# Sums of the moving operand by accumulating DMAs: the last product of an RWKV attention and Hadamard feed-forward kernel

## The chip, the cores and the metric

The kernel runs on one core of a Trainium2 chip. A core has TensorE (PE in the profile) for matmuls, VectorE (DVE), ScalarE (ACT), GpSimd (POOL) and SyncE (SP), which here only issues DMAs. Data live in SBUF, 128 partitions wide; matmuls write into PSUM, eight banks of 128x512 fp32. DMA engines move data between HBM and SBUF, or within SBUF. The engines run their own instruction queues in order and meet at semaphores. The metric is the device time of one execution in microseconds, lower is better; where several executions are known, their median.

## The reference

The input x is 4 x 2048 x 512. It is normalised over channels. An RWKV-v4 attention mixes each token with the one before, forms r, k, v by three 512x512 products, runs the WKV recurrence along time, and multiplies sigmoid(r) * wkv by Wo. A feed-forward forms silu(xn W1) * (xn W3), 2048 wide, applies a Walsh-Hadamard transform to it, and multiplies by W2. Both are added to x:

```python
    hidden = jax.nn.silu(up_gate) * up_lin
    hidden = fwht(hidden)
    out = jnp.einsum('bsh,dh->bsd', hidden, W2)
    ...
    x = x + _L0_attn_ref(xn, ...) + _L0_ffn_ref(xn, L0_ffn_W1, L0_ffn_W2, L0_ffn_W3)
```

All is fp32.

## The kernel before, in words

Tokens are worked in eight blocks of 1024 (`TB`), each in two halves of 512 (`H`). Channels lie on the partitions. A block has three stages: the projections r, k, v, the feed-forward's first two products (`up`, sixteen tiles), and the last product (`down`). The Hadamard transform is folded into W2 once, in the first block (`fold_products`, `fold_butterflies`), so that `down` is one product: the 2048 hidden channels and the 512 channels of sigmoid(r) * wkv, stacked, against W2 and Wo, stacked. The two summands of the output thus come out of the same accumulation.

Each large product uses a scheme with seven block products instead of eight. Its operands are cut into quarters: the weights by halves of input and output channels, the moving operand into y11, y12, y21, y22, by halves of the input channels (first index) and of the tokens (second). The scheme needs sums and differences ("forms") of quarters on both sides. The weights' seven forms are made once by GpSimd (`seven_forms`), stored in HBM (`down_w`), and loaded again for each block (`load_down`, two buffers). The moving operand's forms are made in each block, in place.

In `down`, the moving operand lies in `hid` (sixteen rows of 128 channels) and `r_sb` (four rows). A quarter is a list of pieces: eight rows of `hid`, by twos, and two rows of `r_sb`, one token half of each (`rows`, line 488). A product (`product`, line 498) runs two output tiles of ten 128x512 fp32 matmuls; the profile records each as two. The tuple `order` (line 494) tells which weight form each of the seven products uses. `difference` (line 515) makes the moving operand's forms on VectorE, five subtractions each, in place: y11 becomes y12 - y11 after product 0, y12 becomes y22 - y12 and y22 becomes y22 - y11 between products 2 and 4, y21 becomes y21 - y22 after that. Other VectorE and ScalarE instructions read the banks, add residuals of x from SBUF slots (`stage`, in v_sb; `x22_of`, in e1), and SP stores the results (`store`, line 526).

The order of every engine's queue is the order in which the program issues its instructions: the wrapper `InOrder` (line 24, through which all instructions get line 34 in the profile) keeps it. While `down` runs, the generator `next_tokens` (line 689) prepares the next block, one step ahead of each product: statistics of the new tokens (with a power function on GpSimd, line 130, and a way through HBM), the normalisation (`normalize`, line 145, half of it on GpSimd), the token mixing (`mixed`) and its forms. The loads of the next weight form are issued by SP at the start of each product (line 502) and those of residuals between them.

The final steps of `wkv` (line 221) leave sigmoid(r) * wkv in r_sb; the last instructions of an `up` tile (lines 414 to 419) leave the hidden values in `hid`.

Of the kernel before, what the change touches and what calls it, by code (L numbers as in the profile page):

```python
# [10 lines left out]
ALU = mybir.AluOpType  # L11
# [4 lines left out]
H = 512  # L16
# [23 lines left out]
def tile_rwkv_attn_hadamard_ffn(  # L40
# [15 lines left out]
    NT, C = x.shape  # L56
    F = 2 * w2.shape[1] * P
    NB = C // P
    KH = NB // 2
    NF = F // P  # L60
# [28 lines left out]
    def bank():  # L89
        turn[0] += 1  # L90
        return banks[(turn[0] - 1) % 8]
# [126 lines left out]
            act.copy(dst, pt)  # L218


    def wkv(h):
        w_h, u_h = weff[:, h : h + 1], vec[:, 4, h : h + 1]
        r, k, v = r_sb[:, h, :], k_sb[:, h, :], v_sb[:, h, :]
        a0, a1, b0, b1 = sa[:, OFF - 1 : OFF - 1 + TB], sa[:, OFF : OFF + TB], sb[:, OFF - 1 : OFF - 1 + TB], sb[:, OFF : OFF + TB]
        first_a, first_b, last_a, last_b = a0[:, 0:1], b0[:, 0:1], a1[:, TB - 1 : TB], b1[:, TB - 1 : TB]
        tt, stt, scan, copy = dve.tensor_tensor, dve.scalar_tensor_tensor, dve.tensor_tensor_scan, dve.tensor_copy
        cy = [carry[:, h, n : n + 1] for n in range(3)]

        def exp(t):
            act.activation(t, t, AF.Exp)  # L230


        copy(first_a, cy[0])
        scan(a1, w_h.to_broadcast([P, TB]), k, first_a, ALU.add, ALU.max)
        tt(b1, k, a1, ALU.subtract)
        yield
        stt(e1b, a0, w_h, a1, ALU.add, ALU.subtract)
        stt(e1, k, u_h, a0, ALU.add, ALU.max)
        stt(k, k, u_h, e1, ALU.add, ALU.subtract)
        tt(e1, a0, e1, ALU.subtract)  # L240
        copy(cy[0], last_a)
        yield
        exp(b1)
        exp(e1b)
        yield

        copy(first_a, cy[1])
        tt(a1, b1, v, ALU.mult)
        scan(a1, e1b, a1, first_a, ALU.mult, ALU.add)
        copy(cy[1], last_a)  # L250
        yield
        exp(k)
        exp(e1)
        yield
        copy(first_b, cy[2])
        scan(b1, e1b, b1, first_b, ALU.mult, ALU.add)
        copy(cy[2], last_b)
        tt(v, k, v, ALU.mult)
        yield
        num, den = e1, e1b  # L260
        tt(den, e1, b0, ALU.mult)
        tt(den, den, k, ALU.add)
        dve.reciprocal(den[:, 0:H], den[:, 0:H])
        yield
        dve.reciprocal(den[:, H:TB], den[:, H:TB])
        yield
        tt(num, e1, a0, ALU.mult)
        tt(num, num, v, ALU.add)
        stt(r, r, 1.0, num, ALU.add, ALU.mult)
        stt(r, r, 0.5, den, ALU.mult, ALU.mult)  # L270
        yield


# [64 lines left out]
    def seven_forms(t, a11, a12, a22, a21):  # L338

        sub = ALU.subtract  # L340
        pool.tensor_tensor(t[1], a21, a22, ALU.add)
        pool.tensor_tensor(t[2], t[1], a11, sub)
        pool.tensor_tensor(t[3], a12, t[2], sub)
        pool.tensor_tensor(t[0], a11, a21, sub)

    def forms_in(t):
        seven_forms([t[:, n] for n in range(3, 7)], *(t[:, n] for n in range(4)))

# [47 lines left out]
    def up(i, j, w, tail, step):  # L396

        keep_parts(i, 3 * KH + j, w)
        h0, h1 = hid[:, j, 0:H], hid[:, j, H:TB]

        def on11(pa):
            act.activation(h0, pa, AF.Tanh, scale=0.5)

        def on22(pa, pb, s5):
            dve.scalar_tensor_tensor(h0, h0, 1.0, pa, ALU.add, ALU.mult)
            step()
            dve.tensor_tensor(pb, pb, s5, ALU.add)

        def on12(pc, s5):
            dve.tensor_tensor(pc, pc, s5, ALU.add)  # L410
            step()

        pb, pc, pd = seven(f"{i}_{j}", w, right_of["up"], tail, on11, on22, on12)
        return (
            lambda: act.activation(h1, pc, AF.Tanh, scale=0.5),
            lambda: dve.tensor_tensor(h0, h0, pd, ALU.mult),
            lambda: dve.scalar_tensor_tensor(h1, h1, 1.0, pc, ALU.add, ALU.mult),
            lambda: dve.tensor_tensor(h1, h1, pb, ALU.mult),
        )


# [22 lines left out]
    def fold_butterflies():  # L444

        at, spare = list(fold), e1
        s = 1
        while s < NP:
            for a in range(NP):
                if a & s:  # L450
                    continue
                xa, xb = at[a], at[a | s]
                dve.tensor_tensor(spare, xa, xb, ALU.subtract)
                dve.tensor_tensor(xa, xa, xb, ALU.add)
                at[a | s], spare = spare, xb
            s *= 2
        for a in range(NP):
            x0, x1 = at[a][:, 0:C], at[a][:, C : 2 * C]
            dve.tensor_tensor(spare[:, 0:C], x0, x1, ALU.add)
            dve.tensor_tensor(spare[:, C : 2 * C], x0, x1, ALU.subtract)  # L460
            at[a], spare = spare, at[a]
        return sorted(enumerate(at), key=lambda p: p[1] is not e1)

# [6 lines left out]
    def down_forms(j, at, t):  # L470
        n, a = at[j] if j < NP else (j, None)
        far = down_w[:, :, n].rearrange("f p k c -> p f k c")
        if n < NP:
            a = a.rearrange("p (k m g c) -> p k m g c", k=2, m=2, c=P)
            seven_forms([t[:, f] for f in range(4)], a[:, 0, 0], a[:, 1, 0], a[:, 1, 1], a[:, 0, 1])
            sp.dma_start(out=far[:, 0], in_=a[:, 0, 0])
            sp.dma_start(out=far[:, 1:3], in_=a[:, 1])
            sp.dma_start(out=far[:, 3:7], in_=t[:, 0:4])
        else:
            forms_in(t)  # L480
            sp.dma_start(out=far, in_=t)

    def load_down(i, form):
# [4 lines left out]
    def rows(kh, half):  # L488

        n = NF // 2  # L490
        pieces = [hid[:, kh * n + 2 * a : kh * n + 2 * a + 2, ts(half, H)] for a in range(n // 2)]
        return pieces + [r_sb[:, kh * KH : (kh + 1) * KH, ts(half, H)]]

    order = (0, 1, 4, 6, 5, 3, 2)

    def down(i, w, between, w_after, last):
        y11, y12, y21, y22 = rows(0, 0), rows(0, 1), rows(1, 0), rows(1, 1)
        def product(k, pts, right, start, then):
            if k == 6:
                w_after()  # L500
            elif k:
                w.append(load_down(i, order[k + 1]))
            if k:
                next(between)
            for g in range(KH):
                whole = slice(0, H)
                for pt, cols in ending if last and k == 6 and g == KH - 1 else [(pts[g], whole)]:
                    for n in range(NR):
                        pe.matmul(
                            pt[:, cols], lhsT=w[k][:, n, g, :], rhs=right[n // 2][:, n % 2, cols],  # L510
                            start=start and n == 0, stop=n == NR - 1, skip_group_check=True,
                        )
                    then(g) if cols == whole else c21(g, pt, cols)

        def difference(out, x0, x1):
            for o, p0, p1 in zip(out, x0, x1):
                dve.tensor_tensor(o, p0, p1, ALU.subtract)

        def at(mh, g, half):
            return ts(mh * KH + g, P), ds(i * TB + half * H, H)  # L520
# [7 lines left out]
            sp.dma_start(out=outT[c, t], in_=slot)  # L528

        add = dve.tensor_tensor  # L530
        pa, pb, pc = ([bank() for _ in range(KH)] for _ in range(3))
        ending = [(pb[KH - 1], slice(0, H // 2)), (bank(), slice(H // 2, H))]
        s5 = [small.tile([P, H], F32, tag="s5", name=f"s5_{i}_d{g}") for g in range(KH)]
        for g in range(KH):
            residual(stage[g], 0, g, 0)
        product(0, pa, y11, True, lambda g: act.copy(pb[g], pa[g]))
        difference(y11, y12, y11)

        def c11(g):
            add(stage[g], pa[g], stage[g], ALU.add)  # L540
            store(stage[g], 0, g, 0)
            residual(stage[2 + g], 0, g, 1)
            residual(x22_of[g], 1, g, 1)

        product(1, pa, y21, False, c11)
        product(2, pc, y11, True, lambda g: act.copy(s5[g], pc[g]))
        difference(y12, y22, y12)
        for g in range(KH):
            add(x22_of[g], x22_of[g], s5[g], ALU.add)
        product(3, pc, y22, False, lambda g: None)  # L550
        difference(y22, y22, y11)

        def u2(g):
            act.copy(u2_of[g], pb[g])

        product(4, pb, y22, False, u2)
        difference(y21, y21, y22)
        for g in range(KH):
            add(u2_of[g], u2_of[g], stage[2 + g], ALU.add)
            add(stage[2 + g], pc[g], u2_of[g], ALU.add)  # L560
            store(stage[2 + g], 0, g, 1)
            residual(stage[g], 1, g, 0)

# [205 lines left out]
```

## Time and profile before

| | us |
|---|---|
| median of three runs (lowest, highest) | 3126.11 (3124.63, 3128.18) |
| the profiled execution | 3126.89 |
| its span, first to last instruction | 3125.1 |
| TensorE busy | 3108.2 |
| VectorE busy | 2197.2 |
| ScalarE busy | 873.9 |
| GpSimd busy | 322.6 |
| one product of `down` | 17.17 |
| `down`, seven products | 120.2 |

The span is that of the profiled execution; the execution's own time includes what lies around it. Busy time of an engine is the sum of its instructions; it does not say which engine sets the end, which the chain of waits does. The granted TensorE clock was 0.999 of full speed. All the kernel's own DMAs were issued by SP, on one queue, which moved 333.15 MB; its packets took 30.3% of the time of 16 DMA engines. In the view of stretches, the columns are the stretch, its length, the busy microseconds of PE, the weight loads, DVE, ACT and POOL with their instruction counts, the granted clock, the share of time in which the DMA engines were busy, and GB/s.

### The profile page before, as it was taken

The page shows a single profiled execution, that of the slowest core. Times are in us where ns is not written, and L with a number is a line of the kernel's source. Part 1 is how long each engine was busy: PE and PEld are TensorE (multiplying, and loading weights), DVE is VectorE, ACT ScalarE, POOL GpSimd, SP SyncE. Part 2 cuts the span into 40 slices and gives each one's busy share as a digit, 9 for nine tenths or more (in the row PEclk, how much of TensorE's full clock was granted, in tenths as well). Part 3 has the DMA queues.
Part 4 walks back from the last instruction along what each step waited for, and adds up shares of the span by engine and source line. Part 5 has one row for each costly group of instructions (what it writes and reads, how often), then busy time and mean ns, then how long its engine had stood idle before and what let it go on. Part 6 is the DMA issues. An engine that isn't in the chain of part 4 may idle for free.

```text
span 3125.1 us, 20283 instructions
## 1 busy us (share of the span) xinstructions
PE 3108.2 (99%) x7252; PEld 1378.9 (44%) x7252; DVE 2197.2 (70%) x2317; ACT 873.9 (28%) x1375; POOL 322.6 (10%) x203
## 2 busy tenths in 40 slices
PE   8999999999999999999999999999999999999999
PEld 3444444444444444444444444444444444444444
DVE  6798847876478765797557965589564886658852
ACT  4233023330233203332123321333213331133310
POOL 3353131001100011000110001100011000010000
PEclk9999999999999999999999999999999999999999
DMA  4354433223322242222422233222332224322222
GB/s 163 104 183 162 161 116 110 77 109 135 108 77 76 103 153 96 76 78 107 150 93 78 75 133 123 97 75 79 136 135 78 79 74 160 111 84 73 80 97 78
DMA packets 75813, 334.45 MB, mean 107 GB/s; under 512 B 9152, under 2 KB 18624, under 8 KB 66368
## 3 DMA queue, kind: packets, MB, share of 16 engines
q1 hardware_dynamic: 75712, 333.15, 30.3%
q8 instruction: 58, 0.95, 0.1%
q14 instruction: 43, 0.35, 0.0%
HBM read 286.93 MB, written 46.19 MB: 107 GB/s over the span
## 4 chain that ended last, share of the span: by engine, by line
PE 99%; DVE 0%; DMA 0%; SPq 0%; issue 0%; ACT 0%; ACTq 0%
PE bank L34 99%; DVE xnT L34 0%; DMA hid<-w 0%; DVE tf L34 0%; SPq L34 0%; ACT tf L34 0%; ACT hid L34 0%; DVE v_sb L34 0%; ACTq L34 0%; ACT k_sb L34 0%
## 5 line engine op out<-in xcount | busy, mean ns | idle before, releaser
L34 PE MATMUL bank<-tf,part 128*128 128x512 f32 x2272 | 1042.2, 592 | 0.0
L34 PE MATMUL bank<-hid,dw 128*128 128x512 f32 (+1 forms) x1808 | 787.5, 588 | 0.0
L34 PE MATMUL bank<-xnT,part 128*128 128x512 f32 x1536 | 721.8, 592 | 0.0
L34 PEld LDWEIGHTS bank<-tf,part 128*128 128x128 f32 x2272 | 431.7, 190 | 543.4 <-issue 513.5
L34 ACT COPY bank<-bank 128x512 f32<-128x512 f32 x527 | 300.2, 570 | 1268.1 <-PE bank L34 1243.9
L34 PEld LDWEIGHTS bank<-hid,dw 128*128 128x128 f32 x1808 | 343.5, 190 | 426.0 <-issue 422.8
L34 PEld LDWEIGHTS bank<-xnT,part 128*128 128x128 f32 x1536 | 291.8, 190 | 367.4 <-issue 363.1
L34 DVE TENSOR_TENSOR hid<-hid 128x1024 f32<-128x1024 f32 (+1 forms) x173 | 221.8, 1310 | 105.2 <-PE bank L34 104.3
L34 DVE SCALAR_TENSOR_TENSOR hid<-hid,bank 128x512 f32<-128x512 f32 x256 | 174.0, 680 | 170.8 <-ACT hid L34 170.6
L34 PE MATMUL bank<-hid,part 128*128 128x512 f32 x616 | 271.2, 592 | 0.0
L34 DVE RECIPROCAL e1b<-e1b 128x512 f32<-128x512 f32 x64 | 214.1, 3347 | 1.1
L34 PE MATMUL bank<-r_sb,dw 128*128 128x512 f32 (+1 forms) x452 | 210.7, 588 | 0.0
L34 DVE TENSOR_TENSOR bank<-bank,s 128x512 f32<-128x512 f32 x256 | 168.0, 690 | 36.5 <-ACT bank L34 25.3
L34 ACT ACTIVATE hid<-bank 128x512 f32<-128x512 f32 x272 | 162.2, 600 | 94.0 <-PE bank L34 75.9
L34 PEld LDWEIGHTS bank<-hid,part 128*128 128x128 f32 x616 | 117.0, 190 | 147.3 <-issue 145.7
L34 DVE TENSOR_TENSOR hid<-hid,bank 128x512 f32<-128x512 f32 x256 | 173.6, 678 | 11.5 <-PE bank L34 7.1
L34 POOL TENSOR_TENSOR rs<-rs,neg_half 128x8 f32<-128x8 f32 x7 | 11.5, 1648 | 1581.1 <-DVE rs L34 1581.1
L34 DVE SCALAR_TENSOR_TENSOR hid<-xnT,vec,hid 128x1024 f32<-128x1024 f32 x64 | 93.1, 1489 | 97.2 <-ACT hid L34 97.2
L34 PEld LDWEIGHTS bank<-r_sb,dw 128*128 128x128 f32 x452 | 85.9, 190 | 106.4 <-issue 106.2
L34 ACT COPY s<-bank 128x512 f32<-128x512 f32 x128 | 75.0, 586 | 145.9 <-PE bank L34 145.9
L34 DVE TENSOR_TENSOR v_sb<-bank,v_sb 128x512 f32<-128x512 f32 (+1 forms) x33 | 22.1, 672 | 129.9 <-PE bank L34 129.9
L34 POOL TENSOR_TENSOR tf<-xnT 128x1024 f32<-128x1024 f32 x16 | 46.4, 2902 | 589.9 <-PE bank L34 589.9
(103 smaller groups left out, 2218.0 us busy)
## 6 DMA issues: line engine op xcount, KB each, us to landing
part<-part_w SPq DMA_DIRECT2D x148, 896.0 KB, 4.6
dw<-down_w SPq DMA_DIRECT2D x56, 1280.0 KB, 6.1
part_w<-part SPq DMA_DIRECT2D x22, 896.0 KB, 6.9
k_sb<-x SPq DMA_DIRECT2D x7, 2048.0 KB, 8.3
xnT<-xT SPq DMA_DIRECT2D x7, 2048.0 KB, 9.7
v_sb<-xT SPq DMA_DIRECT2D x48, 256.0 KB, 4.8
out<-v_sb SPq DMA_DIRECT2D x47, 256.0 KB, 2.1
part<-wpart SPq DMA_DIRECT2D x22, 512.0 KB, 5.0
```

What stands on the lines that cost most here:

```text
L34: return self.tc.keep_in_program_order(issue(*args, **kwargs))
```

## The change

The moving operand's forms are no longer made by VectorE but by DMAs that add their source to their destination within SBUF. [...]signs are moved elsewhere: the quarters y12 and y21 are produced negated (`sign`, in the last instruction of `wkv` and of `up`), and the weights' forms are made with the opposite signs where these meet (`signed_forms`, a changed last butterfly, and a few negations on GpSimd in the first block). Each sum (`onto`) is two DMAs on GpSimd's queue, one for the eight rows of `hid` and one for the two of `r_sb`. The products come in another order, and the upper right quadrant of the result is gathered from two pairs of banks instead of one.

```diff
+    def sign(kh, half):
+        return 1.0 if kh == half else -1.0
...
-        stt(r, r, 0.5, den, ALU.mult, ALU.mult)
+        for half in range(2):
+            cols = ts(half, H)
+            stt(r[:, cols], r[:, cols], 0.5 * sign(h // KH, half), den[:, cols], ALU.mult, ALU.mult)
...
+    def signed_forms(t, a11, n12, n22, a21):
+
+        add, sub = ALU.add, ALU.subtract
+        pool.tensor_tensor(t[1], n22, a21, sub)
+        pool.tensor_tensor(t[2], t[1], a11, add)
+        pool.tensor_tensor(t[3], t[2], n12, sub)
+        pool.tensor_tensor(t[0], a11, a21, sub)
+        pool.tensor_scalar(t[2], t[2], -1.0, None, ALU.mult)
...
-            lambda: dve.tensor_tensor(h0, h0, pd, ALU.mult),
+            lambda: dve.scalar_tensor_tensor(h0, h0, sign0, pd, ALU.mult, ALU.mult),
             lambda: dve.scalar_tensor_tensor(h1, h1, 1.0, pc, ALU.add, ALU.mult),
-            lambda: dve.tensor_tensor(h1, h1, pb, ALU.mult),
+            lambda: dve.scalar_tensor_tensor(h1, h1, sign1, pb, ALU.mult, ALU.mult),
...
-            dve.tensor_tensor(spare[:, C : 2 * C], x0, x1, ALU.subtract)
+            dve.tensor_tensor(spare[:, C : 2 * C], x1, x0, ALU.subtract)
...
-            forms_in(t)
+            pool.tensor_scalar(t[:, 1:3], t[:, 1:3], -1.0, None, ALU.mult)
+            signed_forms([t[:, f] for f in range(3, 7)], *(t[:, f] for f in range(4)))
...
-    order = (0, 1, 4, 6, 5, 3, 2)
+    order = (0, 6, 1, 4, 5, 3, 2)
...
-        def difference(out, x0, x1):
-            for o, p0, p1 in zip(out, x0, x1):
-                dve.tensor_tensor(o, p0, p1, ALU.subtract)
+        def onto(kh0, half0, kh1, half1):
+
+            n = NF // 2
+            for t, rows0, rows1 in ((hid, n, n), (r_sb, KH, KH)):
+                out = t[:, kh0 * rows0 : (kh0 + 1) * rows0, ts(half0, H)]
+                pool.dma_start(out=out, in_=t[:, kh1 * rows1 : (kh1 + 1) * rows1, ts(half1, H)], accum_op=ALU.add)
...
-        pa, pb, pc = ([bank() for _ in range(KH)] for _ in range(3))
-        ending = [(pb[KH - 1], slice(0, H // 2)), (bank(), slice(H // 2, H))]
+        pa, pb, pc, pf = ([bank() for _ in range(KH)] for _ in range(4))
+        ending = [(pb[KH - 1], slice(0, H // 2)), (pc[0], slice(H // 2, H))]
...
             residual(stage[g], 0, g, 0)
+            residual(stage[2 + g], 0, g, 1)
         product(0, pa, y11, True, lambda g: act.copy(pb[g], pa[g]))
-        difference(y11, y12, y11)
+        onto(0, 0, 0, 1)
+
+        def c12_part(g):
+            add(stage[2 + g], pc[g], stage[2 + g], ALU.add)
+
+        product(1, pc, y22, True, c12_part)
+        onto(0, 1, 1, 1)
+        onto(1, 1, 0, 0)
 
         def c11(g):
             add(stage[g], pa[g], stage[g], ALU.add)
             store(stage[g], 0, g, 0)
-            residual(stage[2 + g], 0, g, 1)
             residual(x22_of[g], 1, g, 1)
 
-        product(1, pa, y21, False, c11)
-        product(2, pc, y11, True, lambda g: act.copy(s5[g], pc[g]))
-        difference(y12, y22, y12)
+        product(2, pa, y21, False, c11)
+        onto(1, 0, 1, 1)
+
+        def p5(g):
+            act.copy(s5[g], pf[g])
+            add(stage[2 + g], pf[g], stage[2 + g], ALU.add)
+
+        product(3, pf, y11, True, p5)
         for g in range(KH):
             add(x22_of[g], x22_of[g], s5[g], ALU.add)
-        product(3, pc, y22, False, lambda g: None)
-        difference(y22, y22, y11)
...
         product(4, pb, y22, False, u2)
-        difference(y21, y21, y22)
         for g in range(KH):
-            add(u2_of[g], u2_of[g], stage[2 + g], ALU.add)
-            add(stage[2 + g], pc[g], u2_of[g], ALU.add)
+            add(stage[2 + g], stage[2 + g], u2_of[g], ALU.add)
```

More of the change, by code (lines that the diff above doesn't have):

```diff
@@ L399, in up @@
         h0, h1 = hid[:, j, 0:H], hid[:, j, H:TB]
+        sign0, sign1 = (sign(2 * j // NF, half) for half in range(2))
         def on11(pa):
@@ L474, in down_forms @@
             a = a.rearrange("p (k m g c) -> p k m g c", k=2, m=2, c=P)
-            seven_forms([t[:, f] for f in range(4)], a[:, 0, 0], a[:, 1, 0], a[:, 1, 1], a[:, 0, 1])
+            signed_forms([t[:, f] for f in range(4)], a[:, 0, 0], a[:, 1, 0], a[:, 1, 1], a[:, 0, 1])
             sp.dma_start(out=far[:, 0], in_=a[:, 0, 0])
```

## The prediction

> **What bounds the kernel now.** I read the page first: busy times, then the chain that ended last.
>
> ```profile
> span 3125.1 us, 20283 instructions
> PE 3108.2 (99%) x7252; PEld 1378.9 (44%) x7252; DVE 2197.2 (70%) x2317; ACT 873.9 (28%) x1375; POOL 322.6 (10%) x203
> ...
> q1 hardware_dynamic: 75712, 333.15, 30.3%
> ...
> PE 99%; DVE 0%; DMA 0%; SPq 0%; issue 0%; ACT 0%; ACTq 0%
> ```
>
> TensorE is the chain. Busy matmul time alone could hide pipelining gaps, so the view of waits on PE comes second:
>
> ```profile
> engine line waited for: us in total, times, longest us
> PE bank L34 <- DMA hid<-w: 8.9, 1, 8.9
> PE bank L34 <- ACT hid L34: 3.9, 1, 3.9
> PE bank L34 <- DVE tf L34: 0.9, 1, 0.9
> ```
>
> Three waits, 13.7 us, all before 46 us and before any line of the change. From 45.20 us the chain holds 3076.61 us of matmuls without a break. A product of the last stage is 2 output tiles of 20 recorded matmuls; each tile starts 8.58 us after the one before (1078.75 and 1087.33 in the timeline), so a product takes 17.17 us and seven take 120.2 us, in each of eight blocks. Both versions issue the same matmuls (3616 of full width, each recorded as two). So nothing after 45 us can become shorter but the tail behind the last matmul (about 3 us). The change can only hold, or put waits into a gapless TensorE.
>
> The last stage by product, third block, and the three products behind the first, in that block and in the last (columns: stretch, length, busy us of the engines with counts, clock, DMA share, GB/s):
>
> ```profile
> 1078.80:1096.00 17.20, 17.20 (x42) 7.63 (x41) 6.87 (x7) 0.57 (x1) 0.00 (x0) 1.00 0.00 0
> 1096.00:1113.20 17.20, 17.20 (x42) 7.63 (x41) 7.53 (x21) 0.57 (x1) 1.65 (x1) 1.00 0.74 280
> 1113.20:1130.40 17.20, 17.20 (x42) 7.63 (x41) 17.05 (x9) 0.59 (x1) 12.05 (x4) 1.00 0.43 148
> 1130.40:1147.50 17.10, 17.10 (x42) 7.53 (x41) 12.71 (x12) 4.75 (x5) 0.00 (x0) 1.00 0.21 77
> ...
> 1096.00:1147.50 51.50, 51.50 (x122) 22.80 (x121) 37.29 (x41) 5.91 (x7) 13.70 (x5) 1.00 0.46 169
> ...
> 3018.90:3070.40 51.50, 51.50 (x121) 22.80 (x120) 14.56 (x15) 1.62 (x3) 0.00 (x0) 1.00 0.30 107
> ```
>
> To be seen: DVE, which makes the sums now, has room in every stretch but one; the DMA engines are idle during the first product and busiest (0.74) during the second, just where the new transfers begin.
>
> **What the Trainium skill says.** "DMA: Bandwidth & Descriptors", section "SWDGE vs HWDGE vs iDMA": an accumulating DMA can only be issued from GpSimd, whose cores write its descriptors in software; it runs on the same 16 engines as all others. No DMA of this trace comes from GpSimd, so the trace neither confirms nor denies. "Collectives: The Full Stack", section "The bandwidth ceiling: the fold count and why AG ≠ RS ≠ AR": a summing transfer reads two sources for each write and so runs at half a copy's rate, not because the addition costs anything. No run here shows it. "TensorE: Matmul & The Clock Gate", Part 1: after some 3.4 us of idleness TensorE falls to half clock and needs as long to recover. The trace agrees:
>
> ```profile
> 8.86 3.75 PE L34 MATMUL bank<-hid,had_sb 128*128 128x512 f32 x4 [8.86 <-DMA hid<-w]
> ...
> 21.73 12.26 PE L34 MATMUL bank<-tf,w 128*128 128x512 f32 x24 [3.87 <-ACT hid L34]
> ...
> 57.34 10.46 PE L34 MATMUL bank<-hid,w 128*128 128x512 f32 x24
> ```
>
> After 3.87 us of idleness 24 matmuls take 12.26 us, warm ones 10.46: 1.8 us more for each long wait.
>
> **The change part by part.**
>
> Removed: `difference`, four calls of five DVE subtractions of 128x1024, 1.22 us each in the timeline: 20 x 1.22 = 24.4 us a block, 195 us in all. All of it lies under matmuls; worth 0 to the end.
>
> Added on DVE: 32 final steps of `wkv` split in two halves (1.25 us becomes 2 x 0.69: 4 us in all), one more 0.69 us addition per output tile of the upper right quadrant (16 x 0.69 = 11 us), and tensor_tensor replaced by scalar_tensor_tensor in `up` (678 against 680 ns). Cover: DVE is 195 us lighter. Nothing. Added on GpSimd in the first block: 12 small negations at about 1 us, spread over ten tiles of `up` that last 12 us each and where GpSimd has about 8 us of work (eight forms at 0.94 to 0.99 us). Their result is stored and read again only after the fourteenth tile. Nothing. Two output tiles get banks of their own (8 instead of 7): the next block's first banks have been read two products earlier. Nothing. On SP two residual loads move ahead of the first product; the queue is at rest then. Their slots come free with the last `wkv`, before the product. Nothing.
>
> What decides is `onto`. Each of four sums A (y11), B (y12), C (y22), D (y21) is two GpSimd DMAs, hid 128x8x512 (2.10 MB) and r_sb 128x2x512 (0.52 MB), 2.62 MB together. Their order by data: A may start when product 0 has read y11, at 17.2 us of the stage. B overwrites what A reads, so it waits for A. C reads A's result, overwrites what B reads, and waits for B and product 1. D waits for C and product 2. So it is a chain of four, not four parallel transfers. Wanted: A at product 3 (51.5 us), C at product 4 (68.7), B at product 5 (85.8), D at product 6 (103.0). The tight one is C: three sums within 68.7 - 17.2 = 51.5 us. (A alone has 34.3 us. D has as much again behind C.)
>
> GpSimd runs in order. Behind A stands the `pow` of the statistics (1.65 us), so its reader, the store of the statistics on SP, goes when A has been issued. Behind C stands the other half of `normalize` (12.2 us), which now starts when B has landed, instead of at 34.5 us. D, ScalarE's `mixed(1)`, and behind that the copies for product 5 wait for it. From B's landing that takes 12.2 + 4.3 (the mixing) + 1.2 = 17.7 us; product 5 starts one product (17.2) after C has landed, so at least 24 us after B. Hidden, unless issuing a DMA holds GpSimd for many microseconds.
>
> Price of a sum: q1 moved 333.15 MB in 30.3% of 3125.1 us, 352 GB/s while busy. One pass of 2.62 MB at that rate is 7.45 us; with two reads 14.9. At the skill's 436 GB/s (the DMA page, "Anatomy of one DMA", which adds 2.0 us fixed) two passes are an estimated 12.0. I take 13.5, the middle. Of the fixed time I count only the last 2 us, since r_sb's fifth of a sum runs while the next hid part is being released. Other transfers need 0.47 x 51.5 = 24.2 us of the engines in that window, so 27.3 are left (last block: 0.70 x 51.5 = 36.0). Demand: 3 x 13.5 + 2 = 42.5. Product 4 starts 42.5 - 27.3 = 15.2 us late, with re-warming 17.0. Seven blocks: 119; the last, 42.5 - 36.0 + 1.8 = 8.3. Sum +127 on the profiled execution's 3126.9 us (span 3125.1), which stands 0.8 above the median of 3126.1: 3253. Ends of this case: 12.0 gives 10.7 + 1.8 a block and 2 + 1.8 in the last, 3217; 14.9 gives 19.4 + 1.8 and 12.5, 3287. The other weights' loads queue behind no GpSimd wait; they land in 6.1 us and have 17.
>
> **The rivals.** (1) Hidden: an accumulating DMA costs one pass. Then 3 x 7.45 + 2 = 24.4 is below 27.3, and the time is 3126 give or take the 3 us that runs differ by. It decides from 8.4 us a sum downward. For it: the engines have one fully idle product before; two products are left for each sum. Against it: a sum must read two operands, and the margin is 3 us even then. (2) GpSimd is slow: 1024 + 256 rows of 2 KB for each sum need their descriptors written by software. From below that is 0, fully overlapped; no row of the trace bounds it from above. If a sum takes 27 us (generation as long as the transfer, or a summation slower than two passes), the chain of three is 83 us, 32 over, (32 + 1.8) x 8 = 270: 3396. For it: the many short rows. Against it: SP's transfers with rows of a few KB reach 386 to 434 GB/s in the slices of the second product. (3) Between: 8.4 to 12.0 us a sum, stalls of 1 to 11 us, 3135 to 3215.
>
> **How the numbers follow.** Likeliest, two passes: 0.46. Hidden: 0.16 (of it 0.02 for a tail that ends over 6 us earlier, which only a shorter start could give). Between: 0.15. Slow GpSimd: 0.23. A measurement here tells about 0.2% (6 us) from no change. Faster 0.02, same 0.14, slower 0.84. The likeliest one's own range is 3217 to 3287. To hold eight in ten the range takes in the hidden case and part of the slow one: 3122 to 3370.
>
> **What would show it.** Right: matmuls `bank<-hid,dw` that wait for a DMA hid<-hid about eight times, some 10 to 20 us each, at the fifth product of the stage; a chain that holds DMA; PE's busy time near 3120; DVE near 2015 us. GpSimd's queue landing 10 to 20 us for a 2 MB sum. Wrong: no such wait (rival 1), or waits also at the fourth and seventh product (rival 2). My forecast fails if the sums contend less with the loads than work added to work, or if issuing occupies GpSimd long enough to delay `normalize` into product 5.

## The result and the profile after

The changed kernel takes 3250.8 us (median of four runs, 3248.2 to 3252.2), the kernel before 3126.3 in the same comparison. The ratio is 1.0397, 95% interval 1.0379 to 1.0415: slower by about 124 us. The profiled execution's span is 3250.3 us, against 3125.1.

The page of the changed kernel, busy times, DMA queues and the chain that ended last:

```profile
span 3250.3 us, 20307 instructions
PE 3139.8 (97%) x7252; PEld 1387.5 (43%) x7252; DVE 1979.0 (61%) x2205; ACT 875.6 (27%) x1375; POOL 414.8 (13%) x279
...
q1 hardware_dynamic: 75712, 333.15, 29.0%
q0 software_dynamic: 41984, 83.89, 14.6%
...
PE 76%; DMA 15%; DVE 1%; issue 0%; POOL 0%; SPq 0%; ACT 0%; POOLq 0%; DVEq 0%
PE bank L34 76%; DMA hid<-hid 9%; DMA r_sb<-r_sb 4%; DMA stat_d<-rs 1%; DMA dw<-down_w 0%; DMA part<-wpart 0%; DVE e1b L34 0%; DMA v_sb<-stat_d 0%; DVE st L34 0%; DVE xnT L34 0%; DVE sa L34 0%; DVE v_sb L34 0%; DVE hid L34 0%; SPq L34 0%; DVE r_sb L34 0%
```

The same 7252 matmul records; VectorE lost 218 us of work and nothing came of it. The chain, which was all TensorE, now runs through the accumulating DMAs. The new queue q0 moved 83.89 MB (32 sums of 2.62) in 14.6% of 3250.3 us, which is 474.5 us: 177 GB/s, half of q1's 353. What TensorE waited for (us in total, times, longest):

```profile
PE bank L34 <- DMA hid<-hid: 56.2, 7, 13.7
PE bank L34 <- DMA dw<-down_w: 27.5, 7, 7.8
PE bank L34 <- DMA part<-wpart: 10.0, 3, 7.6
PE bank L34 <- DMA hid<-w: 8.2, 1, 8.2
```

All waits of PE, with three small ones, make 107.2 us against 13.7 before: 93.5 more. The rest of the 125.2 us is in PE's busy time, up by 31.6, most of it because the array runs slower for some microseconds after twelve new waits of more than 3 us. Three places in the timeline of the changed kernel show it: two waits for the third sum and a wait for weights (start, length, line, idle time before):

```profile
1204.27 8.71 PE L34 MATMUL bank<-hid,dw 128*128 128x512 f32 x16 [12.52 <-DMA hid<-hid]
...
2403.05 10.07 PE L34 MATMUL bank<-hid,dw 128*128 128x512 f32 x16 [13.73 <-DMA hid<-hid]
...
2779.18 9.72 PE L34 MATMUL bank<-hid,dw 128*128 128x512 f32 x16 [5.57 <-DMA dw<-down_w]
```

Sixteen matmuls take 7.03 us when the array is warm; here 8.7 to 10.1.

How full the DMA engines are while this happens is read from the stretch between the start of product 1 and that of product 4, in the third block (stretch, length, busy us by engine, clock, DMA share, GB/s):

```profile
1139.10:1204.30 65.20, 51.90 (x122) 22.53 (x120) 14.42 (x15) 6.12 (x7) 18.88 (x11) 0.92 1.05 260
```

The stretch lasts 65.2 us instead of 51.5, and the DMA share is 1.05 instead of 0.46. The share adds up the times of all packets, and packets of two queues can overlap, so it can exceed 1. At 1.05 the engines have, on average, no free time left.

Where the time came, by the start of product 0 in each block (us from the start of the span):

| | first product of the last stage, block 0 | from block to block | last start to end |
|---|---|---|---|
| before | 309.7 | 384.5 each | 123.7 |
| after | 323.6 | 397.2, 401.1, 399.9, 398.5, 400.0, 401.6, 399.4 | 129.0 |
| added | 13.9 | 12.7, 16.6, 15.4, 14.0, 15.5, 17.1, 14.9 | 5.3 |

So seven last products lost 106 us together, the eighth 5, and the first block lost 14 before its last product began. Here and below, blocks and products count from 0 where a number is given: the "third block" is block 2, and "product 4" is the fifth.

### The profile page after: what moved, and what is told of

It reads as the page before. It is cut to its first block, busy times and chain, and to the rows that moved or that the text cites. A ratio compares the mean times of both kernels' runs of the same rounds, so it can differ in the third digit from the quotient of the medians.

```text
span 3250.3 us, 20307 instructions
## 1 busy us (share of the span) xinstructions
PE 3139.8 (97%) x7252; PEld 1387.5 (43%) x7252; DVE 1979.0 (61%) x2205; ACT 875.6 (27%) x1375; POOL 414.8 (13%) x279
## 3 DMA queue, kind: packets, MB, share of 16 engines
q0 software_dynamic: 41984, 83.89, 14.6%
## 4 chain that ended last, share of the span: by engine, by line
PE 76%; DMA 15%; DVE 1%; issue 0%; POOL 0%; SPq 0%; ACT 0%; POOLq 0%; DVEq 0%
PE bank L34 76%; DMA hid<-hid 9%; DMA r_sb<-r_sb 4%; DMA stat_d<-rs 1%; DMA dw<-down_w 0%; DMA part<-wpart 0%; DVE e1b L34 0%; DMA v_sb<-stat_d 0%; DVE st L34 0%; DVE xnT L34 0%; DVE sa L34 0%; DVE v_sb L34 0%; DVE hid L34 0%; SPq L34 0%; DVE r_sb L34 0%
## 5 line engine op out<-in xcount | busy, mean ns | idle before, releaser
L34 PE MATMUL bank<-hid,dw 128*128 128x512 f32 (+1 forms) x1808 | 812.6, 603 | 83.8 <-DMA hid<-hid 56.2
L34 PEld LDWEIGHTS bank<-hid,dw 128*128 128x128 f32 x1808 | 351.2, 195 | 529.5 <-issue 465.1
L34 DVE SCALAR_TENSOR_TENSOR hid<-hid,bank 128x512 f32<-128x512 f32 x512 | 332.1, 679 | 192.0 <-ACT hid L34 180.4
L34 POOL DMA_DIRECT2D hid<-hid x32 | 50.5, 1579 | 2084.9 <-PE bank L34 1780.2
L34 DVE TENSOR_TENSOR v_sb<-bank,v_sb 128x512 f32<-128x512 f32 (+1 forms) x65 | 43.1, 679 | 219.2 <-PE bank L34 199.8
L34 ACT ACTIVATE tf<-xnT,omm 128x1024 f32<-128x1024 f32 (+1 forms) x36 | 37.8, 1054 | 408.6 <-DVE xnT L34 263.0
L34 DVE SCALAR_TENSOR_TENSOR tf<-xnT,vec,tf 128x1024 f32<-128x1024 f32 (+1 forms) x36 | 49.6, 1393 | 129.7 <-ACT tf L34 129.4
L34 POOL TENSOR_TENSOR part<-part 128x256 f32<-128x256 f32 x88 | 86.6, 995 | 144.1 <-DMA part<-wpart 103.9
## 6 DMA issues: line engine op xcount, KB each, us to landing
hid<-hid POOLq DMA_DIRECT2D x32, 2048.0 KB, 19.6
```

The source lines that it names most:

```text
L34: return self.tc.keep_in_program_order(issue(*args, **kwargs))
```

## The experiments

**The sums back on VectorE.** The four sums of a block are made by VectorE additions; signs, signed forms, order and banks stay.

```diff
-        def onto(kh0, half0, kh1, half1):
-
-            n = NF // 2
-            for t, rows0, rows1 in ((hid, n, n), (r_sb, KH, KH)):
-                ...
-                pool.dma_start(out=out, in_=..., accum_op=ALU.add)
+        def onto(kh0, half0, kh1, half1):
+
+            for o, p in zip(rows(kh0, half0), rows(kh1, half1)):
+                dve.tensor_tensor(o, o, p, ALU.add)
```

> The changed kernel with its four sums made by VectorE additions instead of accumulating DMAs; signs, forms, order of products and banks stay. My theory (the DMAs cost the time in the last product, and the added negations on GpSimd make the first block about 14 us late): 3140 us, 3136 to 3145. Rival (order, banks or moved residual loads cost something): 3160 or more. Rival (the first block costs nothing, as the prediction said): 3126.

Measured: 3144.3 us, ratio 1.0058 (1.0043 to 1.0073). Some 107 of the 124 us are gone with the DMAs. The rest is in the first block: its last product starts at 323.6 us, as in the changed kernel, and takes 5 us more than before, with one wait of 3.3 us of TensorE for VectorE. Later blocks follow each other by 384.5 us, but one by 385.4. So order, banks and moved residual loads cost nothing to be seen in the later blocks; whether the 5 us in the first are theirs is not shown.

**Copies for sums.** The same DMAs, waits and bytes, but without the addition, so the sums are left out.

```diff
-                pool.dma_start(out=out, in_=..., accum_op=ALU.add)
+                pool.dma_start(out=out, in_=...)
```

> The changed kernel with the same GpSimd DMAs, same bytes and same waits, but copying instead of adding: the sums are left out. My theory (a sum costs two passes of the DMA engines, a copy one): the chain of three lands before product 4, time 3140 to 3155 us, and the share of the engines for this queue halves against 14.6% of the span. Rival (descriptors written by GpSimd, or the latency of its queue, sets the 20 us a sum takes): still 3230 or more.

Measured: 3151.1 us, ratio 1.0086 (1.0070 to 1.0101). The queues of this kernel:

```profile
q1 hardware_dynamic: 75712, 333.15, 29.6%
q0 software_dynamic: 21504, 83.89, 7.4%
```

The same 83.89 MB with half the packets and half the engine time, 7.4% of the span of 3158.3 us: 359 GB/s. An hid part lands in 13.1 us at the median instead of 19.6. No wait for a sum is left. That is the factor of two that was priced as two passes. That the second pass is a second read isn't shown by a run. One rival is a fixed cost for each packet, since the sums have twice as many. The packet records of the traces speak against it: a 2 KB packet takes an engine 0.185 us in the summing queue (mean), 0.094 us in SP's queue (to and from HBM), and a 4 KB packet of the copying queue 0.182. Descriptors written by GpSimd are not the limit either: GpSimd writes for the same rows in both kernels, and in the changed one the engines are full. What the copies still cost lies nearly all in the first block, with 8.8 of the 12.1 us of waits for weights that are left; SP's part in these waits is taken up below, with the statistics.

**No chain.** All three early sums take y21 as their source, so that none waits for another.

```diff
-        onto(0, 0, 0, 1)
+        onto(0, 0, 1, 0)
...
-        onto(0, 1, 1, 1)
-        onto(1, 1, 0, 0)
+        onto(0, 1, 1, 0)
+        onto(1, 1, 1, 0)
```

> The changed kernel with the sources of the first three sums set to y21, so that none waits for another one; bytes and number of DMAs stay (the computed values are other ones). My theory (the DMA engines are full, so what counts is the work and not the order): product 4 is late nearly as much, 3220 to 3250 us. Rival (each link of the chain pays a latency before the next can start, and this makes the lateness): 3140 to 3165 us.

Measured: 3249.7 us, ratio 1.0394 (1.0377 to 1.0411), no difference from the changed kernel. But the waits changed their name:

```profile
PE bank L34 <- DMA dw<-down_w: 77.1, 15, 10.0
PE bank L34 <- DMA part<-wpart: 9.5, 3, 7.6
PE bank L34 <- DMA hid<-w: 8.4, 1, 8.4
PE bank L34 <- ACT hid L34: 3.9, 1, 3.9
PE bank L34 <- DMA hid<-hid: 1.5, 1, 1.5
```

Without the order A, B, C, the loads of weights that share the engines come late instead of the sums. The same stretch as above, from product 1 to product 4 of the third block, is as long and as full as with the chain:

```profile
1145.20:1209.70 64.50, 54.58 (x122) 23.56 (x120) 24.08 (x19) 6.22 (x7) 24.41 (x13) 0.93 1.07 258
```

With or without the chain the same bytes have to pass, and one of them ends last. Which one it is here depends on SP's queue too: SP issues the fourth weight form only when the store of the statistics has landed (1148.8 to 1169.9 us). So the run shows that the chain isn't the cause; it doesn't show that no order of these transfers would be better.

**Half the dose.** Only four of the eight hid rows by DMA, the others and r_sb by VectorE.

```diff
+            m = n // 2
+            out = hid[:, kh0 * n : kh0 * n + m, ts(half0, H)]
+            pool.dma_start(out=out, in_=hid[:, kh1 * n : kh1 * n + m, ts(half1, H)], accum_op=ALU.add)
+            for o, p in list(zip(rows(kh0, half0), rows(kh1, half1)))[m // 2 :]:
+                dve.tensor_tensor(o, o, p, ALU.add)
```

> The changed kernel with four of the eight rows of hid summed by accumulating DMA (1.05 MB a sum instead of 2.62), the others and r_sb by VectorE. My theory: 5.9 us of the engines a sum, 3 x 5.9 + 2 = 20 us, below the 27.3 us left: no lateness, 3138 to 3146 us. Rival (a latency for each sum, whatever its size): 3200 or more.

Measured: 3141.2 us, ratio 1.0048 (1.0033 to 1.0063); no wait for a sum at all. What remains over the kernel before is the first block (its last product starts at 322.9). The stretch of the third block is back at its old length, and the engines have room in it (with the copies above it was 0.93):

```profile
1110.10:1161.60 51.50, 51.50 (x122) 22.80 (x121) 38.35 (x42) 5.55 (x6) 18.30 (x8) 1.00 0.83 229
```

So the DMA sums are hidden up to a size, and the latency of a sum as such is not what costs.

**A transfer less beside them.** The load of the next block's channels is left out; later blocks therefore work on wrong tokens.

```diff
             token_before(i + 1)
-            load_channels(i + 1)
```

> The changed kernel without the load of the next block's channels (2.1 MB from HBM in each of seven last products, issued behind product 0; the tokens after the first block are therefore wrong ones). My theory (work added to work on full DMA engines): 2.1 MB at 352 GB/s is 6.0 us less in seven blocks, 42 us, so 3200 to 3215 us. Rival (latency of the chain of sums alone): 3240 to 3251 us.

Measured: 3200.7 us, ratio 1.0234 (1.0210 to 1.0259), so 50 us less than the changed kernel. Seven loads of 2.1 MB are 6.0 us of the engines each, 42 in all; 7.1 were gained for each. This fits full engines: taking away a transfer that TensorE waits for only a stage later brings its whole engine time, and a little more. The edit does a second thing: the store of the statistics, which stood behind this load on SP's queue, lands in 10.6 us instead of 20.9, and the waits for weights shrink from 27.5 to 1.4 us. That this alone would not have helped is what the run with the statistics on another queue, below, says.

**Only hid by DMA.** r_sb's fifth of each sum goes to VectorE.

```diff
-            for t, rows0, rows1 in ((hid, n, n), (r_sb, KH, KH)):
+            out = hid[:, kh0 * n : (kh0 + 1) * n, ts(half0, H)]
+            pool.dma_start(out=out, in_=hid[:, kh1 * n : (kh1 + 1) * n, ts(half1, H)], accum_op=ALU.add)
+            o, p = rows(kh0, half0)[-1], rows(kh1, half1)[-1]
+            dve.tensor_tensor(o, o, p, ALU.add)
```

> The changed kernel with only hid's part of each sum by accumulating DMA (2.10 MB instead of 2.62), r_sb's on VectorE. My theory (work added to work): three sums take 3 x 3.0 = 8.9 us less of the engines, so some 8 to 9 us less in each of eight last products, 3250 - 70 = 3180 us, 3170 to 3195. Rival (r_sb's DMA runs in the gaps of hid's and costs nothing): 3235 to 3250 us.

Measured: 3243.7 us, ratio 1.0375 (1.0360 to 1.0391): only 7 us less, little more than runs differ by. My expectation was wrong and the rival right. Two stretches of the third block, from the end of sum A's hid data to the first hid data of sum B (stretch, length, busy us by engine, clock, DMA share, GB/s), help to see why. First the changed kernel:

```profile
1162.10:1168.20 6.10, 6.10 (x15) 2.66 (x14) 0.00 (x0) 0.00 (x0) 2.77 (x2) 1.00 0.80 197
```

and the one with hid alone:

```profile
1157.80:1164.10 6.30, 6.30 (x16) 2.85 (x15) 0.97 (x1) 0.00 (x0) 1.60 (x1) 1.00 0.78 260
```

Between these two sums of the chain there are some 6 us without hid data, while one DMA's completion and the next one's issue pass. In the changed kernel r_sb's part of A runs in the first 2 us of them (its last packet is at 1164.3), then SP's loads. Without r_sb the gap stays, and SP's loads alone fill it nearly as much. So hid's part of A lands 40.2 us into the last product in both kernels (means of blocks 1 to 6), that of B after 62.1 and 61.8, that of C after 81.8 and 80.3: removing a fifth of the work brings 1.5 us. "Full engines" holds for the stretch up to product 4 as a whole (its share is still 0.99 here), but work that fits into the gaps of the chain costs little.

**The statistics on another queue.** In the changed kernel SP holds the load of the fourth weight form back behind the statistics: the 8 KB store lands in 20.9 us (median; 2.5 before), and the spread load that follows waits for it. The store stands behind the 2 MB load of the next channels on the same queue and beside a running sum; without that load it took 10.6 us (the run above), so the load makes about half of it. SP's part of the timeline in the third block:

```profile
1142.64 0.38 SPq L34 DMA_DIRECT2D stat_d<-rs  x1
1163.55 0.34 SPq L34 DMA_DIRECT2D v_sb<-stat_d  x1
1163.98 0.80 SPq L34 DMA_DIRECT2D dw<-down_w  x1
```

```diff
-        sp.dma_start(out=stat_d[i]..., in_=rs)
-        sp.dma_start(out=spread, in_=stat_d[i]...)
+        act.dma_start(out=stat_d[i]..., in_=rs)
+        act.dma_start(out=spread, in_=stat_d[i]...)
```

> The changed kernel with the two DMAs of the statistics on ScalarE's queue, so that SP does not hold back the weights' loads behind the landing of an 8 KB store. My theory (the third sum sets the start of product 4; a wait before it only eats part of that wait): the waits for weights go, the waits for the sum grow by as much, 3238 to 3251 us. Rival (the waits for weights, 27.5 us and about 8 us of re-warming, are a cost of their own): 3210 to 3220 us.

Measured: 3270.3 us, ratio 1.0453 (1.0432 to 1.0474): 19 us slower than the changed kernel, outside both expectations. TensorE's waits:

```profile
PE bank L34 <- DMA hid<-hid: 108.2, 8, 17.6
PE bank L34 <- DMA part<-wpart: 9.4, 3, 7.5
PE bank L34 <- DMA hid<-w: 7.8, 1, 7.8
PE bank L34 <- ACT hid L34: 4.4, 1, 4.4
PE bank L34 <- DMA dw<-down_w: 1.5, 1, 1.5
```

The direction is as I had it: the waits for weights vanish, and the waits for the sum take their place. They took more than their place (108.2 against 56.2 + 27.5). The fourth weight form is now issued at 1158.2 us, 34.5 us into the last product; in the changed kernel it was 42.1 us (1164.0). The hid part of sum A lands 30.0 us after its issue at 1139.6 instead of 24.3. It may be that the held-back load had left the engines to the sums. Whether the earlier loads or the third queue as such made the kernel slower wasn't tried.

**The first block.** With the sums on VectorE the first block's 14 us stand alone. Three edits of that kernel: the twelve negations left out (the weights' signs are then wrong), the negations on ScalarE, and the next tile's weights loaded ahead of the forms' store.

```diff
         pool.tensor_tensor(t[0], a11, a21, sub)
-        pool.tensor_scalar(t[2], t[2], -1.0, None, ALU.mult)
...
-            pool.tensor_scalar(t[:, 1:3], t[:, 1:3], -1.0, None, ALU.mult)
```

> Sums on VectorE, and the twelve negations on GpSimd in the first block left out (the weights' forms then have wrong signs). My theory (the negations, some 17 us of GpSimd time in a round of GpSimd and SP that already takes 12 to 15 us a tile, make the first block late): 3126 us within 5. Rival (the rest of the signed forms or the order of products): 3138 to 3146 us.

Measured: 3129.2 us, ratio 1.0007 (0.9999 to 1.0016), and the first block's last product starts at 311.2 us instead of 323.6. The negations are the cause. In the changed kernel they last 15.8 us in all (ten of 1.19, two of 1.97), and the first block is late by nearly that.

```diff
-        pool.tensor_scalar(t[2], t[2], -1.0, None, ALU.mult)
+        act.mul(t[2], t[2], -1.0)
...
-            pool.tensor_scalar(t[:, 1:3], t[:, 1:3], -1.0, None, ALU.mult)
+            act.mul(t[:, 1:3], t[:, 1:3], -1.0)
```

> The changed kernel with the sums on VectorE, and the negations of the weights' forms in the first block on ScalarE instead of GpSimd. My theory (these negations lengthen the round of GpSimd and SP that feeds the first block): 3126 us within 4, no difference from the kernel before. Rival (what makes the first block late is something else of the signed forms): 3136 to 3145 us, as with the negations on GpSimd.

Measured: 3158.5 us, ratio 1.0098 (1.0078 to 1.0119), worse than on GpSimd and outside both expectations. A ScalarE instruction of 0.42 us now stands in its queue until GpSimd has made the form, and behind it stand the bank copies that TensorE needs (nine `df` waits; here two and the PE waits that follow):

```profile
179.22 0.42 ACT L34 ACTIVATE df<-df 128x256 f32<-128x256 f32 x1 [6.65 <-POOL df L34]
...
196.32 0.42 ACT L34 ACTIVATE df<-df 128x256 f32<-128x256 f32 x1 [10.01 <-POOL df L34]
```

```profile
180.27 1.96 PE L34 MATMUL bank<-tf,part 128*128 128x512 f32 x4 [1.49 <-ACT bank L34]
197.37 3.75 PE L34 MATMUL bank<-tf,part 128*128 128x512 f32 x4 [4.85 <-ACT bank L34]
```

The work is lighter, but ScalarE serves TensorE in every tile, GpSimd does not. So this run says nothing for or against GpSimd as the cause; it has a wait of its own.

```diff
+            if j + 2 < NF:
+                parts.append(load_parts(i, 3 * KH + j + 2))
             if i == 0 and j < NR:
                 ...
                 down_forms(j, folded, t)
-            if j + 2 < NF:
-                parts.append(load_parts(i, 3 * KH + j + 2))
```

> Sums on VectorE, negations kept, and in the first block the load of the next tile's weights issued ahead of the store of the forms instead of behind it. My theory (the first block is late because SP holds the load back until GpSimd has made and negated the forms): the round is cut, 3126 us within 5. Rival (GpSimd itself has too much work): 3138 to 3146 us.

Measured: 3170.9 us, ratio 1.0144 (1.0129 to 1.0159), again worse and outside both expectations. The load now stands behind another store on SP, that of the tile's own forms, and goes when that has landed:

```profile
161.48 0.37 SPq L34 DMA_DIRECT2D down_w<-df  x1
161.89 0.51 SPq L34 DMA_DIRECT2D part_w<-part  x1
166.70 0.35 SPq L34 DMA_DIRECT2D part<-wpart  x1
...
180.91 0.37 SPq L34 DMA_DIRECT2D down_w<-df  x1
181.33 0.50 SPq L34 DMA_DIRECT2D part_w<-part  x1
186.11 0.35 SPq L34 DMA_DIRECT2D part<-wpart  x1
```

A tile's round is 19.4 us here, and TensorE needs 12 for a tile. In the changed kernel a round is: forms and negation on GpSimd, their store and the next load on SP (one behind the other), some 6 us of landing, the next forms. That this round is what carries the 15.8 us to TensorE is read from the timeline; my way of cutting it only made a longer one, so it isn't shown by a run.

No experiment points to a version faster than the kernel before, whose TensorE does not wait after 45 us; the best that the DMA sums reach is to be hidden.

## Why the prediction was right, and where it was not

The time: 3253 forecast, 3250.8 measured; slower, as forecast, and within the likeliest case. The mechanism holds: two passes of engines that others use too, and the third sum, or what it displaced, ends after product 4 should have begun. But the sum of the terms was right by luck: the last products were priced some 16 us too high and the first block 14 us too low, and the two errors cancel.

- *The last product.* 17.0 us in each of seven blocks and 8.3 in the last were forecast, 127.3. Measured: 15.2 on average and 5.3, 111.5. The engine time of a sum was 14.8 us (2.62 MB at 177 GB/s), the upper end, not the middle of 13.5 that I took. With 14.8 my formula gives 19.1 us of lateness before re-warming; product 4 was late by 13.1 on average (blocks 1 to 6), so the formula overstates the collision by 6. Other traffic did not give way: between products 1 and 4 SP's packets took 24.6 us of the engines, 24.2 before. (The 0.47 of the forecast is the mean of the blocks; the line shown there has 0.46.) But packets overlap, and 67.7 us of packet times passed in 64.6: that is 3.1. The 2 us for the last landing did not come on top. And of the sums' 44.4 us only 43.1 lay in the stretch; r_sb's part of C can still run when product 4 begins.
- *Weights' loads.* "The other weights' loads queue behind no GpSimd wait; they land in 6.1 us and have 17" failed. They land in 9.8 us at the median, and SP holds one of them back behind the statistics' store, so 27.5 us of the waits bear their name. That costs little by itself: with these waits taken away the waits for the sum grew by more. Product 4 was set by the engines' work and not by one of the two transfers, as the kernel without the chain shows.
- *Re-warming.* 1.8 us for each wait was a little too low. Read from the starts of the matmuls that follow, the twelve long waits lost 1.6 to 3.0 us each, 2.2 on average; the rest of PE's 31.6 us is mostly 0.17 us for each wait, where the end of the last matmul before it is no longer overlapped by the next one. The rule of the Trainium skill, "TensorE: Matmul & The Clock Gate", Part 1 (half clock after about 3.4 us of idleness), agrees with these matmuls of 8.7 to 10.1 us for 7.03. The 3.4 us are no sharp bound here, as far as idle time is read rightly from a profile: 8.8 us also followed an idle time of 3.3 us (changed kernel) and 8.7 one of 2.3 (copies), but only 7.1 followed one of 2.5 (hid alone).
- *Negations in the first block.* "Nothing" was the plain miss: 13.9 us. I compared GpSimd's work in a tile (8 us) with a tile's length (12). The forms, however, are in a round with SP's queue and the landing of the next load. In the kernel before, SP's stores of the forms already follow each other by 13.8, 15.6 and 15.6 us (153.1 to 198.1), more than a tile. As I read it, there was no room for what GpSimd added, free as it was by its busy time.
- *Chain and gap.* That r_sb's part runs while hid's next part is being released was in the forecast, and the kernel with hid alone agrees: it gained only 7 us. I then forgot it in the expectation of that run.
- *The signs.* About eight waits of 10 to 20 us for a sum were named; there were seven, of 3.2 to 13.7, three above 10. Waits at the fourth product were named as a sign of rival 2; they came in four blocks (5.3 to 7.8 us), but for a weight form and not for a sum. PE's busy time was to be near 3120 and was 3139.8; VectorE's 2015, and was 1979.0.
- *GpSimd's issuing.* Rival 2 falls: a sum's two DMAs take GpSimd 1.6 and 1.2 us in the timeline, copies with as many rows land on time, and the engines are full while the sums run. Rival 1 falls as well, since the queue ran at half the rate; yet its threshold (8.4 us a sum) fits both the copies, at 7.3 us, and half the dose, at some 6 us. `normalize`, put behind the third sum on GpSimd, cost nothing to be seen.
- *The Trainium skill.* "Collectives: The Full Stack", section "The bandwidth ceiling: the fold count and why AG ≠ RS ≠ AR", says it of a summing transfer between cores (ReduceScatter): half a copy's rate, for its two reads. Here, within one core's SBUF, the half is measured: 177 against 359 GB/s for the same bytes on the same queue. The two reads as its reason are the page's; no run here shows them.

## What to carry to other kernels

Work taken from an engine that is not the bound brought nothing here; what it is replaced by has to be asked for its own bound, here DMA engines that are busy 30% of the time on average and 0.74 in the very stretch that needs them. Price an accumulating DMA at two passes of its bytes, add it to what else moves in the window between producer and consumer, and compare with the window; here that sum was 6 us too high, and on the safe side. And an engine with a low busy share may still have no room at all, as the first block suggests, when its work is one leg of a round with a queue and a landing time: look at the round's period, not at the share.

## What the runs showed of the hardware that I had not expected

- An 8 KB store, issued behind a 2 MB load and beside a running sum, landed in 20.9 us instead of 2.5; in 10.6 when the load was left out, and in 11.8 on a queue of its own. So a small transfer here paid for the load in front of it and again for the sum beside it.
- The accumulating DMA has twice the packets of the copy (41984 against 21504 for 83.89 MB).
- Freeing a load from a queue in which it stood too long made the kernel 19 us slower; the sum that TensorE awaited landed later. Why is open between the earlier load and the additional queue.
